# Pair inputs of one row group in four moved from VectorE to ScalarE in five row tiles, and a shorter pause between gather bursts in the planner

## The chip, the cores and the metric

The kernel runs on one core of a Trainium2 chip. The metric is the device time of one execution in microseconds (us), from launch to end; lower is better. The engines are called PE (TensorE), DVE (VectorE), ACT (ScalarE), POOL (GpSimd) and SP (SyncE, which here only issues transfers). PEld is PE's weight load.

## The reference

The input x is 4 x 512 x 512. Four residual blocks follow each other, each on a layer-normed x: a sparse attention ("a"), a gated feed-forward network, a differential attention ("b"), and the same feed-forward network again.

The part that this case is about is the similarity inside attention a, which decides for each row which 51 of the 512 columns it may attend to. For every pair (i, j) of the 512 rows of a batch entry it runs a small network:

```
h    = einsum('bsd,fd->bsf', xn, W1)                       # 128 features
pair = relu(h[:, :, None, :] - h[:, None, :, :] + b1)      # 512 x 512 x 128
pair = relu(einsum('bijf,gf->bijg', pair, W2) + b2)        # 64 features
sim  = einsum('bijg,og->bijo', pair, W3)[..., 0] + b3[0]   # one number a pair
_, top_idx = top_k(sim, 51)
```

Attention a then runs its softmax over those 51 columns alone, for which the keys and values of those columns are gathered.

## The kernel before, in words

**Pairs.** A batch entry b has 512 rows, in four row tiles of 128 (`it` from 0 to 3). A row tile is 16 steps `k`, and a step has four row groups `g`, each of two rows (i1 and i1 + 16). Thus `pair_group(b, it, k, g)` runs 256 times for a batch entry and 1024 times in all. It makes the pair input `m` (128 features x two rows x 512 columns, in fp32) by two DVE minima of the row of column features `hw` with a per-partition scalar, multiplies it with `w2s` on PE into the PSUM tile `z`, and takes relu with a per-partition bias from `zb` on ACT into `r`. The minimum replaces relu: relu(a - b) = a - min(a, b), and the a-part is folded into the bias `zb`. To keep fp32 precision at fp16 speed, `hw` holds every value as a pair of fp16 numbers, and PE makes three fp16 products (high by high, and the two mixed ones) for each of the two rows: six matmuls of 64 output columns, two rows side by side in the two halves of the array. `pair_sums` reduces four `r` with the W3 vector on PE (fp32, four 32-column parts side by side) into the tile `sim`, and after 16 steps the row tile's `sims` is copied out by ACT and its diagonal zeroed by POOL.

**Top-k and gathers.** `topk_tile` works on one row tile of `sims`. Seven rounds of DVE max, max_index and match_replace find eight columns each. A round's columns are fetched in two bursts of four gathers: POOL issues one indirect DMA for each of the 51 columns, the first burst of a round with indices from `ix`, the second with indices from `idx`, a copy that DVE makes. A row tile thus has 51 gathers in 13 bursts, into `g` tiles of 13 columns (five buffers). DVE then multiplies by the query, adds, takes the softmax (exp on ACT) and the weighted sum, into `ao`. When the four `ao` of an entry are there, `out_a` transposes and projects them (`aop`, `op`), adds them into the residual `X`, and the entry goes on to its feed-forward network (`f0` for entry 0), attention b (`b0`), second network (`e0`).

**What sets the order.** Nothing is issued as written. `Plan` records every operation with its engine, a cost and its dependencies, and then lists them by an own event model with priorities from several passes; each engine executes its list strictly in order, and semaphores hold it wherever data or a buffer is not ready. The generators only say what may interleave: the pairs of entry 0 run with the preparation of entry 1 and of the weight scales; then the pairs of entries 1 to 3 run beside the dense layers of entries 0 to 2; then the dense layers of the last entries alone. `plan.behind = (tuple(gathered), PAUSE)` adds a dependency for planning only: the next max_index or index copy is not planned before the previous burst of gathers has been issued and PAUSE microseconds have passed. It becomes no wait on the chip; it only shapes the order.

**What the steps below speak of.** `m` has 6 buffers, `z` 7 PSUM buffers, `r` 10, `g` 5, `sims` 2, `idx` 1, and `X` 2. `phase_a(b)` makes `hw`, `zb`, the scales `m1`, the queries `q` and, in HBM, the keys and values `kv`; `hc` in it is the fp32 array (column features, and column features plus b1) that `hw` is split from. All records of the profile carry line 327, the planner's issuing line (329 in the changed kernel), so rows are told apart by tile names.

Of the kernel before, what the change touches and what calls it, by code (L numbers as in the profile page):

```python
# [11 lines left out]
F32 = mybir.dt.float32  # L12
F16 = mybir.dt.float16
I32 = mybir.dt.int32
U32 = mybir.dt.uint32
AF = mybir.ActivationFunctionType
ALU = mybir.AluOpType
# [4 lines left out]
B, S, D = 4, 512, 512  # L22
# [4 lines left out]
TOPK = 51  # L27
ROUNDS = (TOPK + 7) // 8
GROUPS = (13, 13, 13, 12)
PAUSE = 1.0  # L30
EPS = 1e-5
FH = 5
R_BUFS = 10
# [297 lines left out]
def hybrid_block(ctx: ExitStack, tc: tile.TileContext, I, out):  # L331
# [8 lines left out]
    T, A, V, P, SP = plan.engines  # L340
# [5 lines left out]
    fp = ctx.enter_context(tc.tile_pool(name="ffn", bufs=2))  # L346

    def const(name, shape, dt=F32, pool=None):
        return (pool or cpool).tile(shape, dt, name=name, tag=name)
# [4 lines left out]
    def pzt(name):  # L354
        return ps.tile([128, 512], F32, name=name, tag="z", bufs=7)
# [4 lines left out]
    def acct(name):  # L360
        return ps.tile([128, 512], F32, name=name, tag="z", bufs=7)
# [4 lines left out]
    def mm(o, l, r, st, sp):  # L366
        T.matmul(o, l, r, start=st, stop=sp)
# [15 lines left out]
    w2t = const("w2t", [128, 64])  # L383
# [12 lines left out]
    s_gu, s_d, s_a, s_p, s_w = (sc[:, i : i + 1] for i in range(5))  # L396
    c_tanh, c_down, c_exp, c_proj, c_kv, w_up, w_dn, c_nexp = (sc[:, i : i + 1] for i in range(5, 13))
    w2s = const("w2s", [128, 2, 64], F16)
# [128 lines left out]
    st_a = {}  # L527

    def phase_a(b):
# [16 lines left out]
        mv = fp.tile([128, NT, 2], F32, name=f"ln0_{b}mv", tag="lnmv", bufs=2)  # L546
        rs = fp.tile([128, 8, NT], F32, name=f"ln0_{b}rs", tag="lnrs", bufs=2)
        n = 2 if b == 0 else NT
        for t0 in range(0, NT, n):
            ts = range(t0, t0 + n)  # L550
            a, c, r1, r, nb, na = (rs[:, i, t0 : t0 + n] for i in range(6))
# [35 lines left out]
        m1 = pp.tile([128, 8], F32, name=f"hm{b}", tag="hm", bufs=3)  # L587
# [11 lines left out]
        tr, hc = tr[:, 0:2], tr[:, 2:4]  # L599
# [3 lines left out]
        hw = pp.tile([128, 2, S], F32, name=f"hw{b}", tag="hw", bufs=2)  # L603
# [10 lines left out]
        zb = pp.tile([128, 256], F32, name=f"zb{b}", tag="zb", bufs=2)  # L614
        V.tensor_scalar(zb, zp[:, 0:256], -1.0, m1[:, 4:5], ALU.mult, ALU.add)
        w3 = pp.tile([128, 47], F32, name=f"w3{b}", tag="w3", bufs=3)
# [4 lines left out]
        q = pp.tile([128, NT, 64], F32, name=f"q{b}", tag="q", bufs=3)  # L621
# [6 lines left out]
            V.tensor_tensor(kv[:, t, :], qp[:, 64:192], bqkv[:, 64:192], ALU.add)  # L628
            yield 1
        SP.dma_start(kv_d[b].rearrange("(t p) e -> p t e", p=128), kv)  # L630
        st_a[b] = (hw, zb, w3, q)


    sims = {}
# [4 lines left out]

    def pair_group(b, it, k, g):  # L640

        hw, zb, _, _ = st_a[b]
        i1 = it * 128 + g * 32 + k
        m = pp.tile([128, 2, S], F32, name=f"m{b}_{i1}", tag="m", bufs=6)
        z = acct(f"z{b}_{i1}") if b == 0 and g % 2 else pzt(f"z{b}_{i1}")
        r = pp.tile([128, S], F32, name=f"r{b}_{i1}", tag="r", bufs=R_BUFS)

        V.tensor_scalar(m[:, 0, :], hw[:, 0, :], hw[:, 1, i1 : i1 + 1], None, ALU.min)
        V.tensor_scalar(m[:, 1, :], hw[:, 0, :], hw[:, 1, i1 + 16 : i1 + 17], None, ALU.min)
        mv = m.bitcast(F16).rearrange("p a (n t) -> p a n t", t=2)  # L650
        for n, (w, t) in enumerate(((0, 0), (1, 1), (0, 1))):
            for s in range(2):
                mm(z[64 * s : 64 * s + 64, :], w2s[:, w, :], mv[:, s, :, t], n == 0, n == 2)
        c = it * 64 + g * 16 + k
        A.activation(r, z, AF.Relu, bias=zb[:, c : c + 1])
        return r

    sims_open = {}
# [21 lines left out]
    def topk_tile(b, it):  # L680
# [7 lines left out]
        for r in range(ROUNDS):  # L688
            sl = slice(8 * r, 8 * r + 8)
            V.max(vm[:, sl], s)  # L690

            plan.behind = (tuple(gathered), PAUSE)
            V.max_index(ix[:, sl], vm[:, sl], s)
# [3 lines left out]
            for part in range(2):  # L697
# [3 lines left out]
                if part:  # L701

                    plan.behind = (tuple(gathered), PAUSE)
                    V.tensor_copy(idx[:, 4 * r : 4 * r + 4], ix[:, cols[0] : cols[0] + 4])
# [341 lines left out]
    def pairs(b):  # L1046
        last = None
        for it in range(NT):
            for k in range(16):
                row[0] += 1  # L1050
                step_topks()
                rr = []
                for g in range(4):
                    rr.append(pair_group(b, it, k, g))
                    yield 0.65
                    if g == 0 and last:
                        pair_sums(*last)
                        yield 0.86
                last = (b, it, k, rr)
        pair_sums(*last)  # L1060
        yield 0.86
        if b == B - 1:
            step_topks(b)
# [4 lines left out]
    X = {}  # L1068
# [11 lines left out]
    def f2(b):  # L1080
# [4 lines left out]

    prep_w2()
    emit(phase_a(0))
    emit(weave((pairs(0), 1, 0), (serial(lambda: phase_a(1), prep_scales, prep_lambda), 0.3, 0)))
    main = serial(lambda: pairs(1), lambda: pairs(2), lambda: pairs(3))
    side = serial(  # L1090
        lambda: start(0),
        lambda: weave((f1(0, first=True)(), 1, 0), (phase_a(2), 0.2, 20)),
        at(0, first=True),
        lambda: weave((f2(0)(), 1, 0), (phase_a(3), 0.2, 20)),
# [61 lines left out]
```

## Time and profile before

| what | value |
|---|---|
| timed runs | 2690.49, 2700.50 and 2700.76 us, median 2700.5 us |
| the profiled execution | 2689.28 us, span from first to last instruction 2687.6 us |
| granted PE clock, mean | 0.993 |
| PE busy | 2589.3 us, 96% of the span |
| DVE busy | 2133.5 us, 79% |
| ACT busy | 1434.0 us, 53% |
| POOL busy | 1005.9 us, 37% |
| end of the row tiles (`sims` copied out), entry 0 | 119.7, 176.5, 265.5 and 347.8 us |
| the same, entry 1 | 436.7, 527.2, 705.6 and 853.4 us |
| first matmul of the first feed-forward network (`f0z`) | 534.9 us |

A busy share here is an average over stages with different limits. PE's records overlap, since matmuls are pipelined, so that a PE that is shown as 96% busy is not a PE at its peak. The five row tiles that the change names are the second to the fourth of entry 0 and the first two of entry 1, that is, the stretch from 119.7 to 527.2 us.

### The profile page before, as it was taken

To read this page: it belongs to the slowest core of one execution; us is meant where nothing else is said; L and a number is where in the kernel's file an instruction comes from. 1 tells how busy PE (TensorE), PEld (TensorE's weight loads), DVE (VectorE), ACT (ScalarE), POOL (GpSimd) and SP (SyncE) were. 2 spreads that over 40 slices of the span, in tenths; PEclk is the share of its full clock that TensorE was granted. 3 is DMA by queue.
4 is the path that set the end of the run, shared out by engine and by line. 5 is a ranking of instruction groups with operands and counts; after the bars stand their busy time and mean duration, and the time that the engine had idled before them with its cause. 6 is when DMAs were issued, how large, how long until landed. Compare 5 with 4: busy or idle time off the path is not lost.

```text
span 2687.6 us, 43166 instructions
## 1 busy us (share of the span) xinstructions
PE 2589.3 (96%) x15172; PEld 1031.4 (38%) x15172; DVE 2133.5 (79%) x5385; ACT 1434.0 (53%) x2651; POOL 1005.9 (37%) x877
## 2 busy tenths in 40 slices
PE   7998999999999999999999999999999899999898
PEld 3432332244433334443443423344444444344343
DVE  8899999999979999878787799978666365465332
ACT  7865455455537995434343499734322376466421
POOL 0187777756352453550626124454353000000000
PEclk9999999999999999999999999999999999999999
DMA  8511111256661113335435411034556534543445
GB/s 275 157 42 37 40 38 38 79 164 195 194 193 45 39 51 114 110 125 161 130 99 162 119 24 44 28 111 124 162 191 210 161 111 139 152 132 106 124 134 168
DMA packets 223368, 317.69 MB, mean 118 GB/s; under 512 B 29741, under 2 KB 150637, under 8 KB 222126
## 3 DMA queue, kind: packets, MB, share of 16 engines
q1 hardware_dynamic: 197038, 261.40, 31.1%
q0 software_dynamic: 26112, 53.53, 6.9%
q8 instruction: 119, 1.95, 0.3%
q14 instruction: 99, 0.81, 0.1%
HBM read 263.30 MB, written 51.38 MB: 117 GB/s over the span
## 4 chain that ended last, share of the span: by engine, by line
PE 63%; DVE 15%; POOL 7%; DMA 6%; issue 6%; ACT 2%; SPq 1%; DVEq 0%; another core or an unknown queue 0%; POOLq 0%; ACTq 0%
PE z L327 15%; POOL g L327 7%; DVE m L327 7%; PE sim L327 6%; PE f1z L327 3%; PE e2z L327 3%; PE f3z L327 3%; PE e3z L327 3%; PE f2z L327 3%; PE e1z L327 3%; PE f0z L327 2%; DVE g L327 2%; PE e2a L327 1%; PE f3a L327 1%; PE e3a L327 1%
## 5 line engine op out<-in xcount | busy, mean ns | idle before, releaser
L327 DVE TENSOR_SCALAR m<-hw 128x512 f32<-128x512 f32 x2048 | 881.9, 485 | 36.4 <-PE z L327 26.4
L327 ACT ACTIVATE r<-z,zb 128x512 f32<-128x512 f32 x1024 | 668.7, 696 | 343.7 <-PE z L327 196.9
L327 PE MATMUL z<-m,w2s 128*64 128x512 f16 x6144 | 802.2, 393 | 28.5 <-DVE m L327 21.2
L327 POOL DMA_INDIRECT g<-kv,ix x432 | 483.0, 1118 | 368.4 <-DVE ix L327 208.7
L327 POOL DMA_INDIRECT g<-kv,idx x384 | 480.3, 1251 | 290.5 <-DVE idx L327 162.2
L327 PEld LDWEIGHTS <-w2s 128*64 128x64 f16 x6168 | 333.3, 108 | 586.9 <-issue 289.7
L327 PE MATMUL sim<-r,w 128*32 128x512 f32 x2048 | 380.6, 605 | 2.7 <-ACT r L327 2.6
L327 PEld LDWEIGHTS sim<-r,w 128*32 128x32 f32 x2048 | 57.1, 108 | 138.7 <-issue 117.2
L327 POOL TENSOR_SCALAR_AFFINE_SELECT sims<-sims 128x128 f32<-128x128 f32 x16 | 7.3, 457 | 270.7 <-ACT sims L327 270.6
L327 DVE TENSOR_TENSOR g<-g,sc 128x832 f32<-128x832 f32 (+3 forms) x128 | 98.4, 781 | 0.2
L327 PE MATMUL e2z<-e2xt,e2w 128*128 128x512 f16 x384 | 94.8, 378 | 1.5 <-ACT e2xt L327 1.5
L327 PE MATMUL f3z<-f3xt,f3w 128*128 128x512 f16 x384 | 94.7, 378 | 0.0
L327 PE MATMUL e0z<-e0xt,e0w 128*128 128x512 f16 x384 | 87.1, 379 | 0.0
L327 PE MATMUL f0z<-f0xt,f0w 128*128 128x512 f16 x384 | 86.4, 379 | 0.0
L327 PE MATMUL e3z<-e3xt,e3w 128*128 128x512 f16 x384 | 85.4, 379 | 0.8 <-ACT e3xt L327 0.8
L327 POOL MEMSET b3ks<- 2x2048 f16 x4 | 7.2, 1806 | 210.7 <-PE b2st L327 170.6
L327 PE MATMUL f1z<-f1xt,f1w 128*128 128x512 f16 x384 | 85.6, 379 | 0.0
L327 PE MATMUL e1z<-e1xt,e1w 128*128 128x512 f16 x384 | 85.5, 379 | 0.0
L327 PE MATMUL f2z<-f2xt,f2w 128*128 128x512 f16 x384 | 85.3, 379 | 0.0
L327 DVE MAX8 vm<-sims 128x8 f32<-128x512 f32 x112 | 76.3, 683 | 2.3 <-POOL sims L327 1.8
L327 DVE FIND_INDEX8 ix<-vm,sims 128x8 uint32<-128x512 f32 x112 | 76.3, 681 | 0.0
L327 DVE TENSOR_TENSOR g<-g,q 128x832 f32<-128x832 f32 x64 | 64.1, 1001 | 15.0 <-DMA g<-kv,ix 6.8
(636 smaller groups left out, 3694.6 us busy)
## 6 DMA issues: line engine op xcount, KB each, us to landing
f0wr<-wf SPq DMA_DIRECT2D x48, 256.0 KB
wn<-wgu SPq DMA_DIRECT2D x32, 256.0 KB
wf<-f0w SPq DMA_DIRECT2D x16, 512.0 KB
e0w<-wf SPq DMA_DIRECT2D x16, 512.0 KB
f1w<-wf SPq DMA_DIRECT2D x16, 512.0 KB
e1w<-wf SPq DMA_DIRECT2D x16, 512.0 KB
f2w<-wf SPq DMA_DIRECT2D x16, 512.0 KB
f3w<-wf SPq DMA_DIRECT2D x16, 512.0 KB
```

Of the source, the lines that this page charges most:

```text
L327: getattr(eng, op)(*a, **k)
```

## The change

In the row tiles (b, it) = (0,1), (0,2), (0,3), (1,0) and (1,1), the groups with g = 3 (16 of a tile's 64, 80 in all) no longer use DVE. ACT makes each of the two rows of `m` as relu(-h_j + h_i + b1), with scale -1 and a per-partition bias, from an fp32 copy `h32` of `hc`; PE multiplies it with fp32 weights in one fp32 matmul a row, two in place of six fp16 ones; and the relu into `r` takes the plain bias `m1[:, 4:5]`. For entries 0 and 1 `phase_a` adds the making of `h32`: an ACT copy of 1024 elements a partition and a small DVE product for the weights. `h32` lives in the two buffers of the tag "X", which the residuals use later. The planner's PAUSE goes from 1.0 to 0.3.

```diff
-PAUSE = 1.0
+ACT_TILES = ((0, 1), (0, 2), (0, 3), (1, 0), (1, 1))
+ACT_STEPS = lambda k, g: g == 3
+PAUSE = 0.3
...
-        st_a[b] = (hw, zb, w3, q)
+        h32 = None
+        if any(t[0] == b for t in ACT_TILES):
+
+            h32 = fp.tile([128, 2 * S + 64], F32, name=f"h32_{b}", tag="X", bufs=2)
+            A.copy(h32[:, 0 : 2 * S].rearrange("p (a n) -> p a n", a=2), hc)
+            V.tensor_scalar(h32[:, 2 * S :], w2t, s_w, None, ALU.mult)
+        st_a[b] = (hw, zb, w3, q, h32, m1)
...
-
-        V.tensor_scalar(m[:, 0, :], hw[:, 0, :], hw[:, 1, i1 : i1 + 1], None, ALU.min)
-        V.tensor_scalar(m[:, 1, :], hw[:, 0, :], hw[:, 1, i1 + 16 : i1 + 17], None, ALU.min)
-        mv = m.bitcast(F16).rearrange("p a (n t) -> p a n t", t=2)
-        for n, (w, t) in enumerate(((0, 0), (1, 1), (0, 1))):
+        if (b, it) in ACT_TILES and ACT_STEPS(k, g):
+
             for s in range(2):
-                mm(z[64 * s : 64 * s + 64, :], w2s[:, w, :], mv[:, s, :, t], n == 0, n == 2)
-        c = it * 64 + g * 16 + k
-        A.activation(r, z, AF.Relu, bias=zb[:, c : c + 1])
+                i = S + i1 + 16 * s
+                A.activation(m[:, s, :], h32[:, 0:S], AF.Relu, scale=-1.0, bias=h32[:, i : i + 1])
+                mm(z[64 * s : 64 * s + 64, :], h32[:, 2 * S :], m[:, s, :], True, True)
+            bias = m1[:, 4:5]
+        else:
+
+            V.tensor_scalar(m[:, 0, :], hw[:, 0, :], hw[:, 1, i1 : i1 + 1], None, ALU.min)
+            V.tensor_scalar(m[:, 1, :], hw[:, 0, :], hw[:, 1, i1 + 16 : i1 + 17], None, ALU.min)
+            mv = m.bitcast(F16).rearrange("p a (n t) -> p a n t", t=2)
+            for n, (w, t) in enumerate(((0, 0), (1, 1), (0, 1))):
+                for s in range(2):
+                    mm(z[64 * s : 64 * s + 64, :], w2s[:, w, :], mv[:, s, :, t], n == 0, n == 2)
+            c = it * 64 + g * 16 + k
+            bias = zb[:, c : c + 1]
+        A.activation(r, z, AF.Relu, bias=bias)
         return r
```

More of the change, by code (lines that the diff above doesn't have):

```diff
@@ L640, in pair_group @@
     def pair_group(b, it, k, g):
-        hw, zb, _, _ = st_a[b]
+        hw, zb, _, _, h32, m1 = st_a[b]
         i1 = it * 128 + g * 32 + k
```

## The prediction, made before the changed kernel ran

> **What bounds the kernel now.** I read the windows first. From the first row tile's end to the first feed-forward matmul PE is far from full: four windows that each hold one row tile's 51 gathers, then that whole stretch.
>
> ```profile
> core 0: us, PE busy (x) PEld busy (x) DVE busy (x) ACT busy (x) POOL busy (x), PEclk, DMA share, GB/s
> 123.00:214.00 91.00, 89.53 (x691) 32.77 (x685) 89.31 (x223) 54.80 (x88) 74.13 (x53) 1.00 0.14 40
> 215.00:303.00 88.00, 77.99 (x522) 27.27 (x521) 86.05 (x229) 46.03 (x72) 67.05 (x52) 0.96 0.13 39
> 303.00:392.00 89.00, 82.95 (x540) 27.80 (x540) 87.27 (x208) 45.96 (x70) 69.77 (x54) 0.98 0.13 39
> 393.00:484.00 91.00, 86.30 (x557) 27.78 (x552) 89.61 (x217) 48.62 (x76) 69.59 (x53) 0.96 0.13 37
> ...
> 120.00:535.00 415.00, 387.37 (x2537) 129.96 (x2534) 407.68 (x1025) 220.44 (x343) 319.58 (x245) 0.98 0.15 45
> ```
>
> DVE is busy 98% of it, ACT half. PE's busy time flatters it: where PE runs unhindered, 64 records of z take 7.45 us (0.116 each, 0.69 a group of six) and a set of four sim matmuls about 1.0 us, so a row tile needs 64 x 0.69 + 16 x 1.0 = 60 us of PE, against the 82 to 91 us that tiles take here. Next POOL, groups of instructions from 123 to 484 us (busy, mean ns | idle before, releasers), and its waits:
>
> ```profile
> L327 POOL DMA_INDIRECT g<-kv,idx x96 | 146.9, 1530 | 35.3 <-issue 24.5 <-DVE idx L327 9.0 <-DVE g L327 0.9
> L327 POOL DMA_INDIRECT g<-kv,ix x109 | 132.9, 1219 | 45.9 <-issue 27.5 <-DVE ix L327 16.6 <-DVE m L327 1.5
> ```
>
> 146.9 + 132.9 + 35.3 + 45.9 = 361 us: these 205 gathers and the gaps before them are the whole window. Of the gaps 0.30 us each (61.5 us) is a step from gather to gather; 19.7 us is true waiting for DVE. So POOL is full as well, in series: a row tile of 51 gathers takes 90 us = 69.6 gathers + 15.3 steps + 4.9 waits. And the gathers are slow because of DVE. POOL's timeline, then DVE's, at one place:
>
> ```profile
> 199.37 6.79 POOL L327 DMA_INDIRECT g<-kv,idx  x1 [0.30 <-DVE idx L327]
> 206.47 1.24 POOL L327 DMA_INDIRECT g<-kv,idx  x1 [0.30 <-issue]
> ...
> 199.30 6.04 DVE L327 TENSOR_SCALAR m<-hw 128x512 f32<-128x512 f32 x15
> ```
>
> One gather stands for 6.79 us while 15 minima run back to back, and ends just after them. A gather's least time is 0.952; beside minima it is mostly 1.24 to 1.3; 30 of the 205 take over 1.4 and carry 42.6 us above 1.3. The chain of waits over 123 to 484 us says the same: neither engine alone.
>
> ```profile
> by line: DVE m L327 33.4%; POOL g L327 28.7%; issue 16.5%; DVE g L327 6.2%; DVE ix L327 2.6%; DVE sims L327 2.4%; DVE vm L327 2.3%; DMA g<-kv,idx 2.1%; DVE sc L327 1.9%; PE z L327 1.5%; DMA g<-kv,ix 0.8%; DVE idx L327 0.4%; DVEq L327 0.3%;
> ```
>
> This gather chain of entry 0 (123.5 to 483.5 us) gates ao, op and f0z. After 535 us PE is near full, apart from attention b's DVE-bound parts.
>
> **The change part by part.** *DVE, removed.* 160 minima. A mean of 481 ns overlaps its neighbour; the cadence is 242.6 us / 576 = 0.421 us. So 160 x 0.421 = 67 us leave, 13.5 us a changed tile (54 to 40.5). Laying the two kernels' DVE lists side by side and summing the trace's durations, from the first index of tile (0,0) to the last of (0,3) DVE has 360 us of work before (real: 356) and 308 after: 77 us a tile. That is DVE's floor. The added 64-element product per entry is 0.2 us, in cover.
>
> *POOL, unchanged in number, quicker.* At the least time a tile is 51 x 0.952 = 48.6, + 15.3 steps. Over that, before, 10.6 us a tile is starving (42.6 / 4) and 10.4 the ordinary stretch beside minima. The ordinary part goes with the minima's share of time: 66% of DVE's work before, 54% of an 82 us tile after, so 8.6. The starving part goes with long runs of minima. The order of b=0's gather stretch has 413 of 561 minima in runs of 8 or more before, and 193 of 422 after; in runs of 13 or more 245 against 28. I take 5. Waits I leave at 4.5. Sum 48.6 + 15.3 + 8.6 + 5 + 4.5 = 82 us, above DVE's 77, so POOL still ends the stretch: 90 - 82 = 8 a tile, 4 tiles, 32 us.
>
> A rule is weighed here. The Trainium skill, "SBUF — State Buffer", section "A bandwidth-pool intuition that's wrong (but worth ruling out)", says that while DVE holds the shared port pair GpSimd is wholly blocked until that instruction ends. By it gathers and minima add up: 48.6 + 54 = 103 us a tile before, and 13.5 less after, 54 us over four tiles. The row says 90, and 1.28 beside minima, not standstill; only some runs block entirely. I keep the row's 32 us.
>
> *PAUSE.* It issues nothing. Gathers wait only 4.9 us a tile for indices, so earlier ones can give at most 4 x 4.9 = 20 us. It could also cost: a pace faster than POOL's lets DVE run into its own waits for gathers, with minima and next indices queued behind. In the lists the query product of a gather group stands behind the indices of 0 or 1 later bursts before, and of 0 or 1 after too (4 and 2 at the first groups of (0,1)). I take 0, between +20 of loss and -20 of gain.
>
> *Start.* PE has 472 z matmuls issued ahead of tile (0,0)'s last sum before, 399 after; this stretch is PE-bound (86.97 of 87 us busy from 33 to 120), so the gathers begin 73 x 0.1155 = 8.4 us sooner. Against it the h32 copy stands ahead of hw's on ACT's list: 1.3 us (hw's own cast of 1024 elements takes 1.31) straight on the path to the first minima. Net 7 us gained.
>
> *ACT, added.* 160 activations, 32 a tile. The nearest row, r from PSUM, has a cadence of 0.59 (11 in 6.46 us); from SBUF with a bias pointer no row exists, xl with two pointers takes 0.81. Between 0.59 and 0.81 I take 0.65: 21 us a tile on ACT's 46 to 55, 75 of 82 at worst. Covered by POOL's chain. Were that cover gone, ACT would be next. Behind each new activation stand r's, which sim waits for; with 10 r buffers that delay is absorbed.
>
> *PE, swapped.* Six fp16 matmuls (0.69) for two fp32. No 64-wide fp32 row exists; hp (fp32, 128 wide) takes 3.44 us for four, 0.86 each. Side by side like sim's four (1.0 for four) a group is 0.88; one after the other 1.72. I take 0.88: 3 us a tile on 60, PE has 20 spare. Even at 1.72 it is 76.
>
> *SP.* X0's and X1's loads now wait until h32 is freed. X1's stands late in SP's list with f0's weight loads behind it, but the last fp32 group precedes the first f0z in PE's list and those loads feed later chunks: nothing.
>
> *Afterwards.* f0z stands behind the same 390 groups in both PE lists, and after it PE's work is equal (1995 and 1994 us by these rates), so the gain is carried to the end.
>
> *Sum.* 32 + 7 = 39 us against the profiled run's 2689.3: 2650. Timed runs of before fall at 2690.5 and 2700.6; the median lies 11.2 above the profiled run, so on its level 2700.5 - 39 = 2661. I give 2660.
>
> **The rivals.** *(A) DVE's floor decides* (starving vanishes, waits close): 79 us a tile with 2% idle, 4 x 11 + 7 = 51 us, 2649 on the median's level. For: DVE's list has that much less. Against: at 1.28 beside minima POOL needs more. *(B) POOL is hardly faster*: gathers only lose the 1.8 us of the ordinary part, and the start gain is spent on work that DVE then lacks: 4 x 2 to 4 x 3 = 8 to 12 us, 2690. For: fewer minima still fill every gap beside a gather. Against: the runs are cut. *(C) Slower: ping-pong between DVE and POOL from the shorter PAUSE.* Each burst's index stands behind a product that waits for the burst just issued and its landing. Price: such a wait, seen once at 1.87 us before a query product at 216.5 us, for most of 13 bursts, some 22 us a tile against 8 gained: 4 x 14 = 56, less 7, some 50 us slower, 2750. It decides from 4.5 + 8 = 12.5 us of waits a tile, 1 us a burst. Against: the same lead of indices in both lists. That fp32 halves run one after the other can't do it alone (76 us of PE a tile). That ACT's groups replace nothing is excluded by the lists: 1888 minima for 2048.
>
> **How the numbers follow.** Forecast 0.55, A 0.22, B 0.16, C 0.07. The measurement tells about 0.5%, 13.5 us, so faster means under 2687. B lies at that bound: mostly same, a fourth of it faster. Faster 0.55 + 0.22 + 0.03 = 0.80, same 0.13, slower 0.07. Range: from A on the lower level of runs, 2690.5 - 51 - 3 = 2636, to B, 2688.
>
> **What would show it.** First gather near 116 us; tiles' gathers 80 to 84 us apart; POOL's mean gather down from 1.36 to about 1.2, none near 6 us; f0z near 496; PE at its rate after; ACT m near 0.65 us, the fp32 pair near 0.9. Wrong if gaps before gathers grow past 12 us a tile (C), or the gathers' mean stays above 1.3 (B), or f0z comes early and the end does not.

## The result, and the profile after

The changed kernel took 2714.46 us (median; 2703.01 to 2720.92) beside 2695.58 us (2685.29 to 2702.81) of the kernel before on the same chip: ratio 1.0072, interval 1.0056 to 1.0088. It is 19 us slower; the forecast was 40 us faster. The profiled execution has a span of 2710.8 us, 23.2 us more than before's 2687.6.

The gathers of entry 0 went as forecast; what came behind them did not. These are its four gather tiles (in these tables each engine has its busy time and instruction count, then the granted clock, DMA share and rate):

```profile
core 0: us, PE busy (x) PEld busy (x) DVE busy (x) ACT busy (x) POOL busy (x), PEclk, DMA share, GB/s
117.00:200.00 83.00, 79.12 (x544) 30.43 (x542) 71.35 (x178) 66.70 (x114) 58.78 (x53) 1.00 0.22 63
200.00:287.00 87.00, 84.93 (x564) 33.12 (x560) 84.84 (x203) 73.42 (x122) 67.00 (x54) 1.00 0.25 76
287.00:371.00 84.00, 78.29 (x471) 26.59 (x472) 71.79 (x177) 58.71 (x96) 60.90 (x53) 1.00 0.18 57
371.00:455.00 84.00, 78.49 (x521) 29.77 (x517) 75.16 (x179) 65.55 (x107) 62.13 (x52) 1.00 0.14 41
```

From first gather to last end the tiles take 83.1, 86.0, 83.7 and 80.9 us (before: 91.2, 88.0, 88.6, 89.9); DVE is busy 71 to 85 us of each and no longer the whole. POOL's groups of that stretch (busy us, mean ns, then idle time before and what ended it):

```profile
L329 POOL DMA_INDIRECT g<-kv,ix x108 | 131.1, 1214 | 51.6 <-issue 27.1 <-DVE ix L329 20.2 <-DVE m L329 2.1
L329 POOL DMA_INDIRECT g<-kv,idx x96 | 115.7, 1206 | 38.4 <-issue 25.9 <-DVE idx L329 7.7 <-DVE g L329 3.0
```

131.1 + 115.7 = 246.8 us for 204 gathers, 1.21 us each (before 1.36). Entry 0's last gather ends at 455.1 us (before 483.5), 28 us ahead, of which 17 arrive at the first f0z matmul (518.1 for 534.9). The first f0b stands at 696.6 (727.7), 31 us ahead. Then the lead melts: 18 us of it from f0b to e0z, 12 from f1z to f1b, 8 from f1b to e1z, 15 from e1z to e1b. The first matmul of each stage, before and after, in us:

| first matmul of | f0b | e0z | f1z | f1b | e1z | e1b | e3z |
|---|---|---|---|---|---|---|---|
| before | 727.7 | 1037.4 | 1279.0 | 1439.4 | 1752.4 | 1909.3 | 2550.1 |
| after | 696.6 | 1024.3 | 1266.6 | 1439.1 | 1760.2 | 1931.8 | 2569.7 |

From f1z to f1b after takes 172.5 us for 160.4, from e1z to e1b 171.6 for 156.9, with the same feed-forward in each (the e1z stage has 945 matmul records for 920). On the pages, first of before, then of after, the place shows as VectorE's idle time behind PE:

```profile
L327 DVE TENSOR_SCALAR m<-hw 128x512 f32<-128x512 f32 x2048 | 881.9, 485 | 36.4 <-PE z L327 26.4
L329 DVE TENSOR_SCALAR m<-hw 128x512 f32<-128x512 f32 x1888 | 822.0, 488 | 103.0 <-PE z L329 70.3
L329 PE MATMUL z<-m,w2s 128*64 128x512 f16 x5664 | 772.5, 393 | 20.9 <-ACT r L329 9.0
```

and inside the e1z stage as a single hole. This is the timeline of after, most lines left out, among them all of POOL, SP and weight loads (start us, duration, engine, operation, in brackets the idle time before it and what ended it):

```profile
1814.72 1.06 PE L329 MATMUL sim<-r,w 128*32 128x512 f32 x8
...
1815.72 2.45 PE L329 MATMUL z<-m,w2s 128*64 128x512 f16 x20
...
1817.57 0.69 ACT L329 ACTIVATE e1t<-e1z,sc 128x512 f32<-128x512 f32 x1 [4.61 <-PE z L329]
...
1819.03 0.65 PE L329 MATMUL z<-m,w2s 128*64 128x512 f16 x4 [0.86 <-DVE e1t L329]
...
1820.28 0.41 PE L329 MATMUL z<-m,w2s 128*64 128x512 f16 x1 [0.61 <-issue]
...
1820.99 0.40 PE L329 MATMUL z<-m,w2s 128*64 128x512 f16 x1 [0.30 <-issue]
...
1823.88 3.82 ACT L329 ACTIVATE r<-z,zb 128x512 f32<-128x512 f32 x6 [5.62 <-remote]
1823.88 6.56 DVE L329 TENSOR_SCALAR m<-hw 128x512 f32<-128x512 f32 x16 [4.90 <-remote]
1824.62 5.29 PE L329 MATMUL z<-m,w2s 128*64 128x512 f16 x24 [3.22 <-ACT r L329]
```

Fifty pair matmuls take 14.2 us (1815.72 to 1829.91) where 50 x 0.116 = 5.8 would do. The first group of six was through by about 1816.6, yet ScalarE starts its r at 1823.88 and VectorE its next m in the same instant. "Remote" means that the semaphore's rise is on record just before the wait ends, but that no instruction which raises it ended in the 1.5 us before: the release comes late. PE then waits for r, whose reading frees its PSUM buffers, and afterwards runs at half clock (24 matmuls in 5.29 us; the granted clock is 0.52 from 1824.6 to 1829.9). The waits of the whole of after that ended so (us, times, longest):

```profile
ACT r L329 <- remote: 20.6, 10, 5.6
DVE m L329 <- remote: 19.4, 9, 4.9
ACT f2t L329 <- remote: 13.7, 2, 9.1
DVE f2t L329 <- remote: 5.7, 2, 2.9
ACT m L329 <- remote: 3.8, 2, 2.8
```

and of before, where they were there to be seen as well:

```profile
ACT r L327 <- remote: 9.5, 4, 5.8
DVE m L327 <- remote: 2.8, 3, 1.9
```

### The profile page after: what moved, and what is told of

It reads as the page before. It is cut to its first block, busy times and chain, and to the rows that moved or that the text cites. A ratio compares the mean times of both kernels' runs of the same rounds, so it can differ in the third digit from the quotient of the medians.

```text
span 2710.8 us, 42697 instructions
## 1 busy us (share of the span) xinstructions
PE 2599.8 (96%) x15012; PEld 1047.4 (39%) x15012; DVE 2076.3 (77%) x5227; ACT 1517.2 (56%) x2813; POOL 965.1 (36%) x877
## 4 chain that ended last, share of the span: by engine, by line
PE 79%; DVE 10%; DMA 5%; ACT 3%; issue 2%; another core or an unknown queue 1%; SPq 0%; DVEq 0%; ACTq 0%; POOL 0%
PE z L329 24%; PE sim L329 9%; DVE m L329 4%; PE e3z L329 3%; PE f0z L329 3%; PE f1z L329 3%; PE e1z L329 3%; PE e2z L329 3%; PE f3z L329 3%; PE f2z L329 3%; PE e0z L329 2%; DVE g L329 2%; ACT r L329 1%; PE b2qk L329 1%; PE b0av L329 1%
## 5 line engine op out<-in xcount | busy, mean ns | idle before, releaser
L329 DVE TENSOR_SCALAR m<-hw 128x512 f32<-128x512 f32 x1888 | 822.0, 488 | 103.0 <-PE z L329 70.3
L329 PE MATMUL z<-m,w2s 128*64 128x512 f16 x5664 | 772.5, 393 | 20.9 <-ACT r L329 9.0
L329 ACT ACTIVATE r<-z,zb 128x512 f32<-128x512 f32 x944 | 614.0, 700 | 223.0 <-PE z L329 143.3
L329 POOL DMA_INDIRECT g<-kv,ix x432 | 495.3, 1146 | 387.3 <-DVE ix L329 223.4
L329 POOL DMA_INDIRECT g<-kv,idx x384 | 429.8, 1119 | 284.2 <-DVE idx L329 150.7
L329 PE MATMUL sim<-r,w 128*32 128x512 f32 x2048 | 366.0, 606 | 5.9 <-ACT r L329 5.7
L329 PE MATMUL z<-m,h 128*64 128x512 f32 x320 | 121.0, 604 | 9.5 <-ACT m L329 6.0
L329 ACT ACTIVATE m<-h 128x512 f32<-128x512 f32 x160 | 107.5, 730 | 13.1 <-PE z L329 5.0
```

The lines of the kernel that those rows point to most:

```text
L329: getattr(eng, op)(*a, **k)
```

## The experiments

They ran on five more chips, four or two kernels on each, always beside the kernel before. Which chip it was turned out to be half of the answer, so they are told chip by chip; the first comparison's chip is A. Two theories were carried at the start. P: the pause, costed at nothing, is what costs. R: every new list loses time late, whatever the pause. Later ones were S: the plan is too fast for POOL; L: each list has accidents of its own; and C: the losses belong to the chip. Ratios are against before on the same chip.

### Chip B (before 2709.0 us): the change taken apart

ScalarE groups alone, and the pause alone:

```
- PAUSE = 0.3        (from after)
+ PAUSE = 1.0
```

> The ACT groups alone, PAUSE back at 1.0. Changed against the kernel after: one constant. Two theories of where the changed kernel's gain went (31 us ahead at the first f0b, 20 us behind at f2z). Theory P, the shorter pause re-orders the later stages badly: this run keeps the early gain and does not lose it, so 20 to 35 us faster than before (2660 to 2680). Theory R, any new list loses some tens of us in the later, PE-bound stages, because the ACT groups already force a new list: this run is within 10 us of before or slower, like the changed kernel.

Measured: 2699.81 us, ratio 0.9967 (0.9951 to 0.9982). Only 9 us are gained, as R had it and not P; f0b stands at 696.4 us, as early as in after, and f1z to f1b takes 169.5 us.

```
- PAUSE = 1.0        (from before)
+ PAUSE = 0.3
```

> PAUSE 0.3 alone, no ACT groups. Theory P: without the early gain only the loss is left, 30 to 50 us slower than before (2725 to 2745). Theory R: the early stretch changes little and the later one loses what a new list happens to lose, between 0 and 30 us slower. In both the first f0z comes within 15 us of 535, since DVE's work is unchanged.

Measured: 2797.46 us, ratio 1.0324 (1.0294 to 1.0355), 88 us slower, more than either theory had, although entry 0's gathers end 8 us earlier than in before's first trace (475.6). The short pause is no zero here.

After itself, unchanged:

> The changed kernel once more, for a second trace: do PE's stalls of the first trace (around 1336 and 1821 us) and its stage times repeat? If they belong to the list, the f1z to f1b stage takes about 172 us and e1z to e1b about 171 again. If they are accidents of one execution, those stages take some 160 and 158. Time within 0.3% of 2714.

Measured: 2747.98 us, ratio 1.0153 (1.0118 to 1.0188). The time was not within 0.3% of 2714: the chip takes twice the loss of chip A from the same program, and with the ScalarE groups the short pause costs 2747.98 - 2699.81 = 48 us. The losses lie in the same stages (f1z to f1b 172.0, e1z to e1b 176.4 us), which looked like a property of the list.

The pause short only in the first six row tiles:

```
- PAUSE = 0.3        (from after)
+ PAUSE = lambda b, it: 0.3 if 4 * b + it < 6 else 1.0
...
- plan.behind = (tuple(gathered), PAUSE)          (in both places)
+ plan.behind = (tuple(gathered), PAUSE(b, it))
```

> PAUSE 0.3 for the first six row tiles, 1.0 for the ten later ones, with the ACT groups. Theory P: the early gain stays and the later loss goes, 25 to 40 us faster than before (2655 to 2670). Theory R: no better than the kernel with PAUSE 1.0 everywhere, between 10 us faster and 20 us slower than before.

Measured: 2711.29 us, ratio 1.0009 (0.9994 to 1.0025): none of P's 25 to 40 us. The e1z stage is back at 158.2 us, but f0z stands at 539.2 us, 23 us behind e1's 516.2: on this chip the short pause costs both early and late.

### Chip C (before 2687.7 us): what the plan believes of POOL

With PAUSE 0.3 the planner's gather tile is at least 51 x 1.25 + 13 x 0.3 = 68 us; POOL takes 83. If the trouble is a plan that is too fast (theory S), then a gather cost of 1.47 mends it and one of 1.03 with the old pause brings it about.

```
- "indirect_dma_start": 1.25      (from after, PAUSE 0.3)
+ "indirect_dma_start": 1.47
```

> The ScalarE groups and PAUSE 0.3 as after, but the planner's own cost of one gather is 1.47 us instead of 1.25, so its gather tile (51 gathers, some 13 bursts) is 51 x 1.47 + 13 x 0.3 = 79 us, near the 81 to 86 us that POOL takes, instead of 68. Theory S (the plan is too fast: with PAUSE 0.3 the list is made for a POOL that is 15 us a tile quicker than the real one): the loss of PAUSE 0.3 is gone, ratio to before 0.995 to 1.002. Theory P (the short pause itself, which puts the next index work close behind a burst): as after, 1.008 to 1.016. Theory L (each list has losses of its own that no number of the plan orders): anywhere from 0.99 to 1.02.

Measured: 2663.28 us, ratio 0.9910 (0.9894 to 0.9927), faster than S or P had it.

```
- PAUSE = 0.3 ; "indirect_dma_start": 1.25      (from after)
+ PAUSE = 1.0 ; "indirect_dma_start": 1.03
```

> The ScalarE groups and PAUSE 1.0 as before, but the planner's cost of one gather is 1.03 us, so its gather tile is 51 x 1.03 + 13 x 1.0 = 66 us, as fast as after's. Theory S: as slow as after, 1.008 to 1.016. Theory P: as the ScalarE groups alone with PAUSE 1.0, 0.995 to 0.999. Theory L: anywhere from 0.99 to 1.02.

Measured: 2643.25 us, ratio 0.9831 (0.9815 to 0.9847). Theory S falls: the faster plan is the better one. No theory had so low a ratio. It is also the first kernel near the forecast.

```
- PAUSE = 0.3        (from after)
+ PAUSE = 0.65
```

> The ScalarE groups with PAUSE 0.65 (the planner's gather tile 72 us; half way between 68 of after and 77 of PAUSE 1.0). Theories S and P both: between the two, 1.000 to 1.008. Theory L: no order, it may lie outside of the two. Its PE list has short, regular runs of pair matmuls in the stage from e1z to e1b (22 to 30, as PAUSE 1.0), so if it is these runs that decide there, that stage takes 157 to 160 us and not 171 to 176.

Measured: 2661.74 us, ratio 0.9906 (0.9889 to 0.9923): below both ends, 0.997 and 1.015 on chip B, that it was to lie between. (Chip D will put those ends at 0.992 and 0.985, and then it does.) e1z to e1b takes 157.7 us.

```
- PAUSE = 0.3        (from after)
+ PAUSE = 1.4
```

> The ScalarE groups with PAUSE 1.4 (the planner's gather tile 51 x 1.25 + 13 x 1.4 = 82 us, the real one). Theory S: at least as good as PAUSE 1.0, 0.990 to 0.997. Theory P: better still than PAUSE 1.0, below 0.995, as there is more room behind each burst. Theory L: anywhere from 0.99 to 1.02.

Measured: 2681.59 us, ratio 0.9979 (0.9969 to 0.9989), the least gain of the four, and short of what S and P had. None of these four traces has a single "remote" wait, where the four of chip B have 35 to 127 us of them, and f1z to f1b takes 160 to 161 us in them, e1z to e1b 156 to 158.

### Chip D (before 2686.6 us): the same kernels again

Four kernels already timed, unchanged, to part the list from the chip.

> After itself, unchanged, beside three other kernels on one chip. The traces of after show 44 us in which ScalarE or VectorE resume together from a release that no recorded instruction gives (ACT r and DVE m 'remote' 20.6 and 19.4 us), and e5 to e8, on another chip, none at all. Theory L (the losses belong to after's list): ratio 1.007 to 1.016 here too, with such stalls in it and losses of 10 us and more in the f1z and e1z stages. Theory C (they come from the chip or the hour, and only strike some): where the other kernels of this call show no such stalls, after has none either, and its ratio falls to 0.98 to 0.99, as the forecast had it.

Measured: 2646.19 us, ratio 0.9853 (0.9829 to 0.9876). The changed kernel, instruction for instruction the same, is 40.4 us faster here. Its gather tiles take 75.8, 84.9, 82.6 and 79.0 us:

```profile
core 0: us, PE busy (x) PEld busy (x) DVE busy (x) ACT busy (x) POOL busy (x), PEclk, DMA share, GB/s
118.00:194.00 76.00, 75.79 (x541) 30.24 (x538) 70.24 (x179) 65.86 (x113) 59.96 (x53) 1.00 0.24 69
194.00:280.00 86.00, 85.49 (x581) 33.19 (x579) 84.92 (x204) 76.07 (x126) 69.87 (x53) 1.00 0.26 77
280.00:363.00 83.00, 78.72 (x498) 28.42 (x495) 75.51 (x186) 60.97 (x101) 65.43 (x54) 0.98 0.19 57
363.00:442.00 79.00, 78.16 (x524) 29.23 (x522) 76.96 (x183) 64.39 (x107) 61.56 (x52) 1.00 0.16 43
```

and POOL's groups wait for an index 6.1 + 2.4 us where those of chip A waited 20.2 + 7.7, while a gather lasts no less (1.25 us):

```profile
L329 POOL DMA_INDIRECT g<-kv,ix x108 | 137.4, 1272 | 39.2 <-issue 27.2 <-DVE ix L329 6.1 <-DVE m L329 3.4
L329 POOL DMA_INDIRECT g<-kv,idx x96 | 117.3, 1222 | 30.2 <-issue 23.8 <-DVE idx L329 2.4 <-DVE g L329 1.8
```

The fifty pair matmuls of the hole, found by the same sim matmuls ahead of them:

```profile
1762.97 1.06 PE L329 MATMUL sim<-r,w 128*32 128x512 f32 x8
...
1763.96 5.83 PE L329 MATMUL z<-m,w2s 128*64 128x512 f16 x50
1764.88 5.43 ACT L329 ACTIVATE r<-z,zb 128x512 f32<-128x512 f32 x8 [1.27 <-PE z L329]
1764.88 6.42 DVE L329 TENSOR_SCALAR m<-hw 128x512 f32<-128x512 f32 x16 [0.56 <-PE z L329]
```

ScalarE starts its r 0.92 us after the first of them, not 8.16, and PE runs through. A window around the stage, on chip A and then on chip D:

```profile
1760.00:1932.00 172.00, 165.92 (x945) 68.99 (x945) 134.74 (x301) 62.31 (x109) 95.00 (x90) 0.98 0.39 120
1710.00:1872.00 162.00, 162.00 (x946) 67.49 (x946) 134.24 (x302) 64.46 (x110) 101.69 (x90) 1.00 0.43 128
```

and over the whole execution on chip D:

```profile
L329 DVE TENSOR_SCALAR m<-hw 128x512 f32<-128x512 f32 x1888 | 819.6, 488 | 45.7 <-PE z L329 44.9
L329 PE MATMUL z<-m,w2s 128*64 128x512 f16 x5664 | 763.4, 392 | 7.7 <-DVE m L329 4.2
```

VectorE's work is the same to 3 us, its idle time ahead of m is 57 us less; the spans differ by 64.8. Of that difference 20.5 us lie ahead of the first f0z, 40 from f0b to e1b.

> The ScalarE groups with PAUSE 1.0 again (0.9967 on the other chip). Theory L: 0.995 to 0.999 as there, with the f1z stage at a loss of 12 us. Theory C: with no stalls of that kind on this chip 0.985 to 0.99, f1z to f1b about 160 us; with them as before.

Measured: 2662.91 us, ratio 0.9918 (0.9892 to 0.9943), just above theory C's range, f1z to f1b 160.2 us, within it. So on one and the same chip the ScalarE groups bring 2686.57 - 2662.91 = 24 us and the short pause 2662.91 - 2646.19 = 17 us more. POOL's waits beyond the step of 0.30 us are some 10 us a tile with PAUSE 1.0 (before: some 5) and some 2 with 0.3: that is where the pause's gain comes from.

> The ScalarE groups with PAUSE 1.0 and a gather of 1.03 us in the plan again (0.983). Theory L: 0.981 to 0.985 on this chip too, whatever the stalls of the others. Theory C: if after and the ScalarE groups alone show the stalls on this chip, this one does too, and its ratio rises to 0.99 or more.

Measured: 2642.30 us, ratio 0.9841 (0.9816 to 0.9865), as on chip C.

> Before itself, for its trace on the same chip. Ratio 1.00 by all theories. Theory C: as many of these stalls as in the other three; theory L: few, as in its first trace (12 us).

Measured: 2685.02 us, ratio 0.9998 (0.9985 to 1.0010). Its trace has no "remote" wait, nor have the other three of this chip: theory C. As the same list of after gains here and loses on A and B, theory L can't hold for it.

What marks the two kinds of chip, call them late and prompt, can be read in the profile's records of the engines' own semaphores. After has 2805 matmuls that raise PE's. On chip D 2804 raises are recorded; on chip A 2586. Over all twenty traces, before's and after's first ones with them, 164 to 245 of PE's raises are missing in each of the ten of chips A, B and E, and at most 6 in each of the ten of C, D and F. (A missing landing time in the rows of DMA issues is no such mark: seven of the ten traces of prompt chips lack it for gathers too.)

Counted by the time since the last gather was issued, on chip A 344 of the 1300 signals of PE that fell due within 2.5 us of an issue have no record from 0.3 us before to 0.5 us after the matmul's end, and none of the other 1505 lacks one; on chip D it is 10 of the 1993 between first and last gather. VectorE's and ScalarE's signals are alike: 412 of 2027 and 313 of 1153 near an issue on chip A, none later; 0 and 3 on D. The hole above is of this kind: groups ended near 1816.6, 1817.3, 1817.9 and 1819.7 us, and four records stand together at 1823.85 to 1824.08, after five gathers issued from 1815.66 to 1820.70. So on the late chips signals come late, or are lost to the record, in the wake of a gather's issue; where engines stand idle until a late release, as here, the lateness is real.

It also goes with the time lost. The same list on a late chip and on a prompt one, with the "remote" waits of all engines added up (two engines that wait together count twice):

| list | "remote" waits on the late chip, us | span there less span on the prompt chip, us |
|---|---|---|
| before | 12 (A) | 3.5 (D) |
| groups alone | 35 (B) | 32 (D) |
| after | 67 (A), 85 (B), 79 (E) | 65, 87, 98 (D) |
| PAUSE 1.0, gather 1.03 | 89 (E) | 112 (D) |
| pause alone | 127 (B), 109 (E) | 103, 88 (F) |

Chips E and F come next. Each chip was used at one time only, so that chip and hour can't be told apart; and every execution here was recorded by the profiler (each has a granted clock on record), so that the recording itself may have a part in it. No run tests either.

### Chip E (before 2708.0 us): a chip of the late kind again

> Before with PAUSE 0.3 and no ScalarE groups (1.0324 where signals between engines came late). Theory C (the loss is the chip's, the pause in itself is harmless or a gain): on a chip with prompt signals 0.99 to 1.00, with POOL's waits beyond 0.30 us shorter than in before; on one with late signals 1.02 to 1.04 again. Theory P (the short pause makes a ping-pong between VectorE and POOL when VectorE is full): 1.02 or more on any chip.

Measured: 2785.58 us, ratio 1.0283 (1.0252 to 1.0314), with 109 us of "remote" waits; this much both theories had for a late chip.

> After itself, to tell which kind of chip this is. Theory C: 0.984 to 0.988 if its trace shows no release without a record, 1.005 to 1.016 if it shows several.

Measured: 2747.07 us, ratio 1.0150 (1.0117 to 1.0182), with "remote" waits of 35.3 us for ACT r and 19.1 for DVE m, and 2581 of PE's 2805 raises on record: as theory C had it.

> The ScalarE groups with PAUSE 1.0 and a gather of 1.03 us in the plan (0.983 and 0.984 on two chips with prompt signals). If this chip has late signals: theory C with the loss in proportion to the gathers alone, about as after (1.00 to 1.015); theory L (the list decides how much of it is felt), less than after by 0.01 or more. If signals are prompt: 0.982 to 0.986 by both.

Measured: 2745.15 us, ratio 1.0121 (1.0079 to 1.0163), where two prompt chips gave 0.983 and 0.984. Not after's list alone: a different list with the same groups loses as much.

```
- PAUSE = 0.3 ; "indirect_dma_start": 1.25      (from after)
+ PAUSE = 0.3 ; "indirect_dma_start": 1.03
```

> The ScalarE groups with PAUSE 0.3 and a gather of 1.03 us in the plan. If what helps is a plan that hands POOL its next burst early, both together are at least as good as either, 0.978 to 0.985 where signals are prompt; if each list has an accident of its own, anywhere from 0.98 to 1.00.

Measured: 2817.46 us, ratio 1.0406 (1.0352 to 1.0460), the slowest of all. What it gives on a prompt chip, of which the expectation spoke, was not run.

### Chip F (before 2686.2 us): the pause without the groups

> Before with PAUSE 0.3. Where the trace shows no release without a record: 0.985 to 1.00 if the loss on the other chips was theirs, 1.02 or more if the short PAUSE starts a ping-pong of its own when VectorE is full. Where it shows many: 1.025 to 1.035 again.

Measured: 2699.84 us, ratio 1.0050 (1.0025 to 1.0075), with prompt signals. The pause alone costs 14 us even so, between the two ranges. Entry 0's gathers end at 467.5 us, 17 earlier than before's on chip D, but the first f0z stands 12.9 us later (551.0 for 538.1) and the spans differ by 13.3: all of the loss is there by f0z. From 465 to 545 us PE waits 5.6 us for POOL's at, and ScalarE 33.8 us for pair matmuls (before, on chip D, 21.2). The earlier gathers had little to bring without the groups: VectorE has the same work ahead of f0z in both lists (774 minima for 776), busy 511 us for 509. Its idle time there grows from 29.1 to 39.7 us, which is most of the loss. That the shorter pause helps only when the ScalarE groups relieve VectorE is what the four combinations on prompt chips show; which wait starts that idle time was not settled.

> The ScalarE groups with PAUSE 1.4. Where signals are prompt 0.998 again. Where they are late: 0.985 to 1.00 if a longer pause in the plan leaves room for late signals, 1.01 or more if it doesn't.

Measured: 2678.94 us, ratio 0.9973 (0.9961 to 0.9986), as on chip C.

### All runs with the ScalarE groups, by what the plan gives POOL

The tile in the plan is 51 gathers at the plan's cost and 13 pauses, at the least.

| kernel | plan's tile, us | ratio, prompt chips (C, D, F) | ratio, late chips (A, B, E) |
|---|---|---|---|
| PAUSE 0.3, gather 1.03 | 56 | | 1.041 |
| PAUSE 1.0, gather 1.03 | 66 | 0.983, 0.984 | 1.012 |
| after: 0.3, 1.25 | 68 | 0.985 | 1.007, 1.015, 1.015 |
| 0.65, 1.25 | 72 | 0.991 | |
| 0.3 in six tiles, then 1.0; 1.25 | 68, then 77 | | 1.001 |
| groups alone: 1.0, 1.25 | 77 | 0.992 | 0.997 |
| 0.3, 1.47 | 79 | 0.991 | |
| 1.4, 1.25 | 82 | 0.998, 0.997 | |

Nearly in order, and in opposite orders: the faster the plan hands POOL its bursts, the better on a chip with prompt signals and the worse on one with late ones. This is against theory L, and a list's gain on prompt chips is against R; a planned tile of 77 us is the only setting tried on both that beats before on both. On prompt chips PAUSE 1.0 with a gather of 1.03 equals or slightly betters after. What makes a chip late was not found, and whether a run without gathers would lose nothing there was not tried.

## Why the prediction was wrong

Two steps failed: PAUSE at nothing, and "the gain is carried to the end". A third, POOL's waits, was mis-sized, which chip D hides by luck.

- **What bounds the kernel, the removed minima, the start.** Right. The first gather came at 117.2 us (forecast 116), DVE's busy time is (71.35 + 84.84 + 71.79 + 75.16)/4 = 75.8 us a tile (77).
- **POOL's tile at 82 us, and the sum of 39 us.** The tile is met only together with the short pause: 83.4 us on chip A, 80.6 on D (before, on D, 89.6). With the groups alone it is 85.9 on D, since POOL's waits, left at 4.5 us, become some 10. So the part that was priced brings 24 us on D, not 39, and the pause, priced at nothing, 17 more: that after gains 40 us there is luck. The gathers themselves are as priced, 48.6 + 8.6 + 5 = 62 us a tile against 51 x 1.21 = 62. One detail missed: gathers of 5.71 and 4.05 us were left at 319.41 and 408.25 us where none near 6 was expected.
- **The rule that was weighed.** Keeping the row above the estimate of 54 us drawn from the Trainium skill ("SBUF — State Buffer", "A bandwidth-pool intuition that's wrong (but worth ruling out)") was right: on chip D the four tiles of after are 36 us shorter. But that gathers and minima add up in full was the prediction's own reading. The page has GpSimd blocked by a DVE operation in a 2-port mode until that one ends (whether the minima are of that kind no run shows), and a gather's 1.24 to 1.3 us beside minima, for 0.952 at least, is less than one minimum of 0.421 us more; only the long gathers go beyond that.
- **ScalarE's and PE's new work.** Two ScalarE minima in a row take 1.33 us on the timeline, 0.66 each (forecast 0.65); PE's fp32 pairs wait 9.5 us in all on chip A, 0.3 on D.
- **f0z near 496 us.** 497.7 on chip D; 518.1 on A, where 63 us pass from the last gather to f0z for the 51 of before.
- **PAUSE at nothing, 20 us either way.** This term failed. With the groups it is worth 17 us of gain on chip D and costs 48 us on B, both measured against the groups alone; on a late chip it lies far outside the bounds. On chip A itself the pause was not run alone. The bounds were made from POOL's waits for indices, which is where its gain is; the loss lies elsewhere, in engines that stand waiting for each other while gathers are in flight.
- **"The gain is carried to the end."** This step failed on the chip of the comparison. It rested on equal PE work after f0z, and that was so (389 pair groups stand ahead of f0z for 388); what it left out is the time that PE stands or runs at half clock. The lead of 16.8 us at f0z becomes a loss of 23.2 at the end. The f1z and e1z stages take 9.6 and 9.9 us more than the same list's on D, f0b to e0z 9.4 and f1b to e1z 8.2. PE's time at half clock is 46.8 us on A for 30.0 on D, so some 8 of the 65 us between the two chips are paid that way (an estimate: half the difference). On chip D the step holds: f0z comes 40.4 us earlier than before's there and the end 38.1 (2684.1 to 2646.0), though f0b stood 54.5 us ahead in between, and the e1z stage is 5 us longer there too, by the list alone.
- **The rivals.** C had the right sign; its +50 us stands against 19 on chip A and 39 on B and E. But not the place: POOL's waits beyond 0.30 us were forecast to pass 12.5 us a tile and are some 11, 3, 8 and 7. The forecast's own last sign, "f0z comes early and the end does not", is what came true, if with less than half of f0z's lead. (A slip without weight: a fourth of B's 0.16 is 0.04, not 0.03.)
- **What could have been read.** Before's trace had both marks: 12.3 us of "remote" waits, and 2462 of PE's 2691 raises on record. The prediction priced neither.

## What to carry to other kernels

An edit that lets one engine run closer behind another bought its gain here from promptness, so the forecast held only on the chips whose signals were prompt; look in the trace for releases that come long after their instruction before counting on it. Time such an edit on more than one chip: the same instructions stood at 0.985 and 1.015 here. And where a planner's number sets the slack, try it in both directions, since the value that was best with prompt signals lost 1.2% with late ones.

## What was not expected of the hardware

On three chips of six (before at 2695.6, 2709.0 and 2708.0 us for 2686 to 2688 on the others) many of the engines' signals that fall due within 2.5 us of a gather's issue leave no record in time (of PE's 344 of 1300 on chip A, 384 of 1292 on E), and engines wait up to 9.1 us on chip A for a release that comes late; in these two traces none that falls due longer after an issue lacks its record. PE's clock fell to a half behind the hole of chip A (granted clock 0.50 from 1822.9 to 1829.7 us), so part of that stall is paid twice. A gather itself lasts no longer there (1.21 us on A, 1.25 on D).
